# Four-layer 56x56 image kernel: layer 1's last image stored by quarters, other buffers for layer 0's images, first group's channels of two convolutions stored and loaded ahead of the rest

## The chip, the cores and the metric

The kernel runs on one core of one Trainium2 chip. The metric is the device time of one execution in microseconds. The core has five engines, each with its own instruction stream: TensorE (PE in the profile; PEld are its weight loads), VectorE (DVE), ScalarE (ACT), GpSimd (POOL) and SyncE (SP). Data move between DRAM and the on-chip memory (SBUF) by DMAs, which SP, ACT and POOL issue. A DMA that an engine issues stands in that engine's stream, so it goes out only after everything ahead of it there. All queues share the core's 16 DMA engines.

## The reference

The input is 8 images of 56 x 56 pixels with 192 channels, float32. Four layers follow each other, each with a residual:

```
x = x + L0(gn(x))   # p * (toeplitz over w and over h of q*v), then a projection
x = x + L1(gn(x))   # window attention, 7x7 windows shifted by 3, 6 heads
x = x + L2(gn(x))   # projection to 384, 3x3 depthwise conv, decays in 4 directions, projection
x = x + L3(gn(x))   # 7x7 depthwise conv, layer norm, GELU MLP, scaled
```

`gn` is a group norm over each image (32 groups of 6 channels), so no layer can start on an image before that image is finished in the layer before. The shift by 3 rolls the image by three rows and three columns, both when layer 1 reads and when it writes.

## The kernel before

The work is done in stages, one after the other over all 8 images: layer 0's first phase (q and v), layer 0's mixing, layer 1, layer 2's projection in, layer 2's mixing (384 channels in groups of 16), layer 2's projection out with layer 3's input, layer 3's depthwise convolution (192 channels in groups of 16), and layer 3's MLP. Between stages the data go through DRAM: `x1` and `x2` are the images that enter layers 1 and 2, `pd` the projected images of layer 2, `zd` the inputs of layer 3's convolution. Inside a stage a framework adds the waits that data and buffers need and schedules each engine's order of instructions; SP's, ACT's and POOL's DMAs have their places in these streams. Every stage takes its tiles from pools that reuse the memory of earlier stages; a tile that lies on an older tile waits until the readers of that one, its DMAs too, have finished. The program keeps at most eight DMAs of SP and ACT together outstanding: each waits for the one eight before it.

An image lies in a tile of 128 partitions as two halves (partitions 0 to 63 the upper 28 rows, 64 to 127 the lower), with three blocks `j` of 64 channels.

- **Layer 0's mixing** (`layer0_mix`, from L462). Images are loaded into `x0` tiles (L468), the first before anything else; the products of the Toeplitz rows are copied to `o` (L529, first `o` tile allocated at L522), each image is normalized to `xn` (L474), and an image is stored to `x1` by two DMAs (L481). Behind the last products `loaded()` (L1193) opens a pool of three layer-1 image tiles at the end of the memory and loads images 0 and 1 into it.
- **Layer 1.** `layer1_load` calls `rolled` (L590), which loads an image in 18 DMAs (L598): rows and columns are rolled, so a DMA moves runs of 53 or of 3 elements. An image has 128 x 3 x 28 x 2 = 21,504 such runs, about 2.4 MB. `layer1_norm` writes normalized windows to `xr` (L619), takes their mean with a matmul (L626) and squares (L630); `layer1_weights` folds vectors into the weights (L567, L578), for which POOL has loaded `w_qkv` and `w_proj`. Image b is then done in four quarters `g` of 7 rows each half: scores and softmax, with a mask tile `bm` loaded on SP (L693), then the mix, which adds its result to the image tile in place (L767). After the four quarters the image is stored to `x2` by 18 DMAs (`rolled`, L598). The next images' norms run ahead of time in between.
- **Layer 2's projection in** (`layer2_in`, from L770) for each image: POOL clears borders of an `x2` tile (L774, L775), SP loads the image in two DMAs (L777, L778), DVE normalizes it into `xn` in three instructions (L783), POOL clears borders of `xn` (L786, L787), TensorE projects (`pin`, L795), DVE adds the bias `b_in` into `pt` (L803), and SP stores `pt` to `pd[b]` (5.57 MB, L804). The two `x2` tiles lie on layer 1's image tiles. POOL loads `w_in` and `b_in` (L97) ahead of the first image.
- **Layer 2's mixing** (`layer2_mix`). For a group of 16 channels SP loads the band weights `wt` (2.05 MB, L825) and the group's channels of all 8 images (`zc`, eight DMAs of 0.23 MB, L830); TensorE convolves four channels at a time (`cv`, L839). Two groups' tiles are in flight.
- **Layer 3's convolution** (`convolve`) has the same form with `wt` of 4.2 MB (L1004), `zc` of eight times 0.25 MB (L1009) and TensorE's `cps` (L1016).

## Time and profile before

| | us |
|---|---|
| median of 3 runs | 6279.67 (6277.85 to 6285.88) |
| the profiled execution | 6264.17 |
| its span in the trace | 6262.4 |
| TensorE busy | 5524.5 (88%) |
| VectorE busy | 3441.0 (55%) |
| ScalarE busy | 2243.7 (36%) |
| GpSimd busy | 1312.8 (21%) |

Approximate stages in the trace, with TensorE's busy time:

| stage | window, us | TensorE busy, us |
|---|---|---|
| layer 0, first phase | 60 to 867 | 739.4 |
| layer 0, mixing | 867 to 2137 | 1166.8 |
| layer 1 | 2137 to 3610 | 1194.3 |
| layer 2, projection in | 3610 to 3854 | 242.2 |
| layer 2, mixing | 3854 to 4480 | 590.8 |
| layer 2, projection out | 4480 to 5064 | 431.8 |
| layer 3, convolution | 5064 to 5376 | 299.9 |
| layer 3, MLP | 5376 to 6262 | 830.6 |

In the lines of the trace the first number is the start in us from the span's start, the second the busy time, then the engine, the line of the source, the operation, the tile written and the tiles read, how many instructions the row joins, and in brackets the idle time of the engine before the row and what ended it. A row that begins with SPq is SP's queue issuing DMAs; its time runs from the first issue to the last, waits between them included. Times of the profiled execution can't be laid beside the median directly: this execution was 15.5 us below it.

### The profile page before, as it was taken

How to read it: one execution, taken by the hardware profiler on the slowest of the kernel's cores; microseconds unless marked ns; L12 is line 12 of the kernel's file. 1: busy time of each engine (PE TensorE's matmuls, PEld its weight loads, DVE VectorE, ACT ScalarE, POOL GpSimd, SP SyncE). 2: the span in 40 equal slices, each digit the busy share in tenths (PEclk: the TensorE clock that was granted, in tenths of full speed). 3: DMA queues.
4: the chain of work that ended last, by engine and by line, in shares of the span. 5: the costliest groups of instructions: out<-in, count | busy, mean ns of one | idle time of the engine just before them, and what ended most of it. 6: DMA issues, size and time to landing. Idle time of an engine off the chain costs nothing. (4 is left out here: it accounts for less than half of the span.)

```text
span 6262.4 us, 126450 instructions
## 1 busy us (share of the span) xinstructions
PE 5524.5 (88%) x55636; PEld 3577.2 (57%) x55636; DVE 3441.0 (55%) x4776; ACT 2243.7 (36%) x2929; POOL 1312.8 (21%) x833
## 2 busy tenths in 40 slices
PE   6899989999999788888888698999688879799999
PEld 5677766666666355445454365777444479544444
DVE  5677766556555344444444386888787710433331
ACT  2334444344444233333333200555355510233333
POOL 1100025444444021121221101333200100110100
PEclk8899999999999798888888798999889989899999
DMA  6799986666665514444432395666666578422210
GB/s 165 188 220 207 192 246 262 256 253 259 254 260 208 77 33 64 56 64 60 59 50 39 55 259 224 215 220 232 190 164 198 165 292 330 154 80 67 71 58 24
DMA packets 1039757, 1013.11 MB, mean 162 GB/s; under 512 B 832281, under 2 KB 964549, under 8 KB 1012325
## 3 DMA queue, kind: packets, MB, share of 16 engines
q1 hardware_dynamic: 1027920, 951.41, 53.6%
q0 software_dynamic: 6416, 34.07, 1.6%
q10 hardware_dynamic: 4868, 19.52, 0.9%
q8 instruction: 437, 7.16, 0.5%
q14 instruction: 116, 0.94, 0.0%
HBM read 676.28 MB, written 345.08 MB: 163 GB/s over the span
## 5 line engine op out<-in xcount | busy, mean ns | idle before, releaser
L371 PE MATMUL qv<-w_qv_sb,xn 64*112 64x288 f32 x5376 | 724.0, 426 | 48.4 <-DVE act L377 45.2
L409 POOL COPY lc<-lt 128x896 f32<-128x896 f32 (+1 forms) x320 | 575.8, 1816 | 623.6 <-PE op L417 605.8
L371 PEld LDWEIGHTS qv<-w_qv_sb,xn 64*112 64x112 f32 x5376 | 534.8, 184 | 232.3 <-DVE act L377 61.2
L378 ACT ACTIVATE act<-act 112x576 f32<-112x576 f32 x448 | 299.5, 682 | 463.0 <-DVE act L377 421.3
L1115 PE MATMUL ph<-y,w_sb 64*128 64x392 f32 x2304 | 399.2, 499 | 6.4 <-ACT hid L1119 6.4
L417 PE MATMUL op<-rc,lc 128*56 128x56 f32 x9216 | 344.1, 223 | 54.4 <-POOL lc L409 29.7
L417 PEld LDWEIGHTS op<-rc,lc 128*56 128x56 f32 x9216 | 312.7, 138 | 137.4 <-issue 72.2
L1126 PE MATMUL po<-hid,w_sb 128*64 128x392 f32 x2304 | 386.3, 494 | 0.0
L429 PE MATMUL pj<-xn,w_p_sb 64*128 64x392 f32 (+1 forms) x1920 | 374.2, 516 | 8.4 <-issue 5.6
L450 PE MATMUL y<-pp,w_o_sb 128*64 128x392 f32 (+1 forms) x1920 | 356.1, 504 | 14.8 <-DVE x L456 6.6
L377 DVE TENSOR_TENSOR act<-qv,b_qv 112x576 f32<-112x576 f32 x448 | 320.5, 750 | 85.5 <-PE qv L371 85.3
L1133 DVE TENSOR_TENSOR x<-x,z 128x392 f32<-128x392 f32 x96 | 72.3, 753 | 520.8 <-ACT z L1131 520.8
L409 ACT COPY rc<-rt 128x896 f32<-128x896 f32 (+1 forms) x160 | 256.8, 1606 | 239.4 <-PE op L417 218.6
L839 PE MATMUL cv<-zc,wt 128*128 128x224 f32 x1536 | 312.8, 355 | 27.9 <-DMA zc<-pd 27.9
L710 POOL TENSOR_TENSOR e<-e,mx 128x1176 f32<-128x1176 f32 x64 | 139.8, 2185 | 920.4 <-DVE mx L709 920.4
L839 PEld LDWEIGHTS cv<-zc,wt 128*128 128x128 f32 x1536 | 290.5, 189 | 71.0 <-issue 54.9
L443 DVE TENSOR_TENSOR pp<-pp,ot 128x784 f32<-128x784 f32 (+1 forms) x160 | 154.6, 966 | 312.8 <-ACT pp L434 293.0
L660 PE MATMUL qk_ps<-xr,wg 64*96 64x392 f32 x1536 | 310.8, 513 | 14.8 <-ACT qk L666 13.3
L1016 PE MATMUL cps<-zc,wt 128*128 128x224 f32 x1536 | 299.9, 356 | 25.3 <-DMA zc<-zd 24.4
L1115 PEld LDWEIGHTS ph<-y,w_sb 64*128 64x128 f32 x2304 | 220.8, 189 | 176.7 <-issue 26.8
L1016 PEld LDWEIGHTS cps<-zc,wt 128*128 128x128 f32 x1536 | 290.0, 189 | 35.2 <-issue 27.5
L852 POOL TENSOR_TENSOR rows<-rows,loc 128x896 f32<-128x896 f32 x96 | 228.3, 2378 | 389.7 <-ACT rows L848 262.4
(207 smaller groups left out, 9293.2 us busy)
## 6 DMA issues: line engine op xcount, KB each, us to landing
lt<-left SPq DMA_DIRECT2D x72, 1792.0 KB
rt<-right SPq DMA_DIRECT2D x72, 1792.0 KB
left<-qv SPq DMA_DIRECT2D x224, 252.0 KB
right<-qv SPq DMA_DIRECT2D x448, 126.0 KB
wt<-in_band_dram SPq DMA_DIRECT2D x24, 2048.0 KB
wt<-in_band_dram SPq DMA_DIRECT2D x12, 4096.0 KB
pd<-pt SPq DMA_DIRECT2D x8, 5568.0 KB
zc<-pd SPq DMA_DIRECT2D x192, 232.0 KB
```

The lines of the kernel that those rows point to most:

```text
L371: nc.tensor.matmul(ps[s][:, which, 0:D1 // 2], xn[64 * s:64 * s + 64, j, bass.ts(i, 2 * W)], w_qv[64 * s:64 * s + 64, j, which, ns], start ...
L377: nc.vector.tensor_tensor(act, ps[s][:, :, 0:D1 // 2], b_qv[:, :, ns], ALU.add)
L378: nc.scalar.activation(act, act, AF.Silu)
L409: copy(c[:, 0:nu], raw.rearrange("p (w u d) -> p u d w", u=nu, d=64 // nu)[:, :, d0:d0 + 8])
L417: nc.tensor.matmul(op[64 * u:64 * u + W, i, :], lc[:, u, i], rc[:, u, i], start=True, stop=True)
L429: nc.tensor.matmul(ps[0:M, s, 0:TT], w_p[64 * s:64 * s + 64, j, d0:d0 + M], xn[64 * s:64 * s + 64, j, ts], start=(j == 0), stop=(j == 2),)
L450: nc.tensor.matmul(y[64 * s:64 * s + 64], w_o[0:M, c, 64 * j:64 * j + 64], pp[0:M, s], start=(c == gated[0][0]), stop=(c == gated[-1][0]),)
L660: nc.tensor.matmul(ps[s], wg[64 * s:64 * s + 64, j, c0:c0 + HC], xw[64 * s:64 * s + 64, j, gs], start=(j == 0), stop=(j == 2),)
L839: nc.tensor.matmul(dst, wt[:, c4 + i, 128 * q:128 * q + 128], zc[:, :, c4 + i, q:q + NPAIR], start=(q == 0), stop=(q == 1),)
L1016: nc.tensor.matmul(dst.rearrange("p (b n) -> p b n", n=NPAIR), wt[:, c4 + i, q * OP:(q + 1) * OP], zc[:, :, c4 + i, q:q + NPAIR], start=(q ...
L1115: nc.tensor.matmul(ps[:, s, 0:TT], w0[64 * s:64 * s + 64, j, m * 128:(m + 1) * 128], y[64 * s:64 * s + 64, j, ts], start=(j == 0), stop=(j ...
L1126: nc.tensor.matmul(ps[64 * s:64 * s + 64], w1[:, m, 64 * j:64 * j + 64], hid[:, m, s], start=(m == 0), stop=(m == 5),)
```

## The change

1. Layer 0's mixing allocates and loads its first image only after the first operand copies and the first `o` tile. The pools place tiles in the order of allocation, so the `x0` tiles move up in memory (their base goes from 32,736 to 108,000 bytes in a partition) and `o` and the operands move down.
2. The layer-1 pool opens with a dummy tile (8 images over 3 buffers). Image 0's loads go out on two queues, block `j` 0 and 2 on SP and 1 on POOL. Image 1's loads are written later in the source, after image 0's norm; in the streams, ten of its 18 loads now stand ahead of the last store of layer 0 and eight behind it.
3. Layer 1's last image is stored in quarters by the new `rolled_rows`, after each quarter's mix: 12, 12, 12 and 18 DMAs on SP.
4. `layer2_in` is split: `layer2_image` allocates, clears and loads. Image 0's load goes to POOL's queue, ahead of `w_in` and `b_in`, which go to ACT's queue. Image b + 1 is asked for before image b is projected. In DVE's stream the first of the three L783 instructions of image 1 now stands ahead of those of image 0, and the other two directly behind them.
5. `pd` of the last image is stored in two DMAs, its first 16 channels (0.24 MB) and the rest. In both convolutions, the first group loads `wt` for 4 channels, then `zc` over three queues (images 0, 3, 6 on SP, 1, 4, 7 on POOL, 2, 5 on ACT), then `wt` for the other 12.

TensorE's stream has the same instructions in the same order as before.

```diff
@@ -482,7 +482,7 @@
                     x1[b].rearrange("(j p) n -> p j n", p=64)[:, :, s * NH:(s + 1) * NH], x[64 * s:64 * s + 64]
                 )
 
-        x, xn, gate, left_over, st = [load(0)], None, iter(()), 0, None
+        x, xn, gate, left_over, st = [], None, iter(()), 0, None
 
         todo = [
             (b, s, d0, len(chunks)) for b in range(nimg) for chunks, subs in PASSES for s in subs
@@ -520,6 +520,9 @@
                         done[1] += 1
 
                 o = pool.tile([120, H, 128], F32, name="o")
+                if not x:
+
+                    x.append(load(0))
                 for at in range(0, 64 // nu * len(subs), 8):
                     right_operand()
                     layer0_products(ops[n % 2], nu, lcs[n], rcs[n])
@@ -587,19 +590,33 @@
         nc.vector.tensor_scalar(wg[:, :, 0:C], wg[:, :, 0:C], HD ** -0.5, None, ALU.mult)
         return wg, bq, w_proj, bpr
 
-    def rolled(dram_image, tile_image, store):
+    def rolled(dram_image, tile_image, store, queues=(nc.sync,)):
 
         d = dram_image.rearrange("(j p) (h w) -> p j h w", p=64, w=W)
         for s, h0, h1, r0 in ((0, 0, 28, 3), (1, 0, 25, 31), (1, 25, 28, 0)):
             for w0, w1, c0 in ((0, 53, 3), (53, 56, 0)):
                 for j in range(3):
+                    eng = queues[j % len(queues)]
                     sb = tile_image[64 * s:64 * s + 64, j, h0:h1, w0:w1]
                     dr = d[:, j, r0:r0 + h1 - h0, c0:c0 + w1 - w0]
-                    nc.sync.dma_start(dr, sb) if store else nc.sync.dma_start(sb, dr)
-
-    def layer1_load(b, pool):
+                    eng.dma_start(dr, sb) if store else eng.dma_start(sb, dr)
+
+    def rolled_rows(dram_image, tile_image, g):
+
+        d = dram_image.rearrange("(j p) (h w) -> p j h w", p=64, w=W)
+        for s in range(2):
+            for h0, h1 in ((7 * g, 7 * g + 7),) if (s, g) != (1, 3) else ((21, 25), (25, 28)):
+                r0 = (28 * s + h0 + 3) % H
+                for w0, w1, c0 in ((0, 53, 3), (53, 56, 0)):
+                    for j in range(3):
+                        nc.sync.dma_start(
+                            d[:, j, r0:r0 + h1 - h0, c0:c0 + w1 - w0],
+                            tile_image[64 * s:64 * s + 64, j, h0:h1, w0:w1],
+                        )
+
+    def layer1_load(b, pool, queues=(nc.sync,)):
         x = pool.tile([128, 3, H // 2, W], F32, name="x1")
-        rolled(x1[b], x, False)
+        rolled(x1[b], x, False, queues)
         return x
 
     def layer1_norm(b, x, pool, psum, consts):
@@ -767,15 +784,18 @@
             nc.vector.scalar_tensor_tensor(xs, ps, bpr[:, j:j + 1], xs, ALU.add, ALU.add)
 
 
-    def layer2_in(b, pool, xpool, psum, w_in, b_in):
-
+    def layer2_image(b, xpool, queue):
 
         x = xpool.tile([128, 3, R2, W], F32, name="x2")
         nc.gpsimd.memset(x[0:64, :, 0], 0.0)
         nc.gpsimd.memset(x[64:128, :, R2 - 3:R2], 0.0)
         src = x2[b].rearrange("(j p) (h w) -> p j h w", p=64, w=W)
-        nc.sync.dma_start(x[0:64, :, 1:R2], src[:, :, 0:R2 - 1])
-        nc.sync.dma_start(x[64:128, :, 0:R2 - 3], src[:, :, R2 - 1:H])
+        queue.dma_start(x[0:64, :, 1:R2], src[:, :, 0:R2 - 1])
+        queue.dma_start(x[64:128, :, 0:R2 - 3], src[:, :, R2 - 1:H])
+        return x
+
+    def layer2_in(b, x, pool, psum, w_in, b_in):
+
         sc, sh = scsh2[:, b, 0], scsh2[:, b, 1]
         xn = pool.tile([128, 3, R2, 64], F32, name="xn2")
         nc.gpsimd.memset(xn[:, :, :, W:64], 0.0)
@@ -801,7 +821,11 @@
             dims = [list(z) for z in pt.ap]
             dst = bass.AP(pt.tensor, pt.offset + i, [dims[0], [nh, ns], [P2, C2]])
             nc.vector.tensor_tensor(dst, ps[:, 0:ns, 0:C2], b_in[:, v, 0:ns], ALU.add)
-        nc.sync.dma_start(pd[b], pt)
+
+        n = CG2 if b + 1 == nimg else 0
+        if n:
+            nc.sync.dma_start(pd[b][:, 0:n], pt[:, 0:n])
+        nc.sync.dma_start(pd[b][:, n:C2], pt[:, n:C2])
 
     def layer2_mix():
 
@@ -822,12 +846,15 @@
             def load(g):
                 cs = slice(g * CG2, (g + 1) * CG2)
                 wt = pool.tile([128, CG2, 256], F32, name="wt2")
-                nc.sync.dma_start(
-                    wt, bass.AP(band.tensor, band.offset + g * CG2 * BL2, [[1, 128], [BL2, CG2], [1, 256]])
-                )
+                src = bass.AP(band.tensor, band.offset + g * CG2 * BL2, [[1, 128], [BL2, CG2], [1, 256]])
+
+                n, queues = (CG2, (nc.sync,)) if g else (4, (nc.sync, nc.gpsimd, nc.scalar))
+                nc.sync.dma_start(wt[:, 0:n], src[:, 0:n])
                 zc = pool.tile([128, nimg, CG2, P2], F32, name="zc2")
                 for b in range(nimg):
-                    nc.sync.dma_start(zc[:, b], pd[b][:, cs])
+                    queues[b % len(queues)].dma_start(zc[:, b], pd[b][:, cs])
+                if n < CG2:
+                    nc.sync.dma_start(wt[:, n:CG2], src[:, n:CG2])
                 return wt, zc
 
             def front(c4, wt, zc, loc, rows, sums):
@@ -1001,12 +1028,15 @@
             for g in range(C // CG):
                 cs = slice(g * CG, g * CG + CG)
                 wt = pool.tile([OP, CG, BAND], F32, name="wt")
-                nc.sync.dma_start(
-                    wt, bass.AP(band.tensor, band.offset + g * CG * BL, [[1, OP], [BL, CG], [1, BAND]])
-                )
+                src = bass.AP(band.tensor, band.offset + g * CG * BL, [[1, OP], [BL, CG], [1, BAND]])
+
+                n, queues = (CG, (nc.sync,)) if g else (4, (nc.sync, nc.gpsimd, nc.scalar))
+                nc.sync.dma_start(wt[:, 0:n], src[:, 0:n])
                 zc = pool.tile([OP, nimg, CG, NB], F32, name="zc")
                 for b in range(nimg):
-                    nc.sync.dma_start(zc[:, b], zd[b][:, cs])
+                    queues[b % len(queues)].dma_start(zc[:, b], zd[b][:, cs])
+                if n < CG:
+                    nc.sync.dma_start(wt[:, n:CG], src[:, n:CG])
                 yc = pool.tile([OP, nimg, CG, NPAIR], F32, name="yc")
                 for c4 in range(0, CG, 4):
                     ps = psum.tile([OP, 2, 512], F32, name="cps")
@@ -1194,7 +1224,10 @@
             raws.close()
             xpool = images.enter_context(tc.tile_pool(reuse_waits="tile", name="l1x", bufs=3, side="right"))
             x.append(xpool)
-            x.extend(layer1_load(b, xpool) for b in range(min(2, nimg)))
+
+            for _ in range(-nimg % 3):
+                xpool.tile([128, 3, H // 2, W], F32, name="x1")
+            x.append(layer1_load(0, xpool, (nc.sync, nc.gpsimd)))
 
         layer0_mix(pool, blocks, psum, ops, w_p, w_o, loaded)
 
@@ -1225,6 +1258,8 @@
         xr = [next(steps)]
         for _ in steps:
             pass
+        if nimg > 1:
+            x.append(layer1_load(1, xpool))
         values = layer1_scores(0, xr[0], pool, psum, S, es, consts)
 
 
@@ -1258,9 +1293,12 @@
                 layer1_mix(g, x[b], values, pool, psum, es, consts)
                 values = following
                 gn_piece(gn[b], x[b].rearrange("p j h w -> p j (h w)"), g)
+                if b + 1 == nimg:
+                    rolled_rows(x2[b], x[b], g)
             for _ in steps:
                 pass
-            rolled(x2[b], x[b], True)
+            if b + 1 < nimg:
+                rolled(x2[b], x[b], True)
         gn_aggregate(gn[nimg - 1], mv2[:, nimg - 1])
     images.close()
 
@@ -1269,10 +1307,13 @@
         xpool = st.enter_context(tc.tile_pool(reuse_waits="tile", name="l2x", bufs=2, side="right"))
         pool = st.enter_context(tc.tile_pool(reuse_waits="tile", name="l2i", bufs=2))
         psum = st.enter_context(tc.tile_pool(reuse_waits="tile", name="l2ip", bufs=4, space=PSUM))
-        w_in = resident("w_in", nc.gpsimd, pool)
-        b_in = resident("b_in", nc.gpsimd, pool)
+        x = [layer2_image(0, xpool, nc.gpsimd)]
+        w_in = resident("w_in", nc.scalar, pool)
+        b_in = resident("b_in", nc.scalar, pool)
         for b in range(nimg):
-            layer2_in(b, pool, xpool, psum, w_in, b_in)
+            if b + 1 < nimg:
+                x.append(layer2_image(b + 1, xpool, nc.sync))
+            layer2_in(b, x[b], pool, psum, w_in, b_in)
             if b == nimg - 3:
                 run(gn_finish(mv2[:, last], scsh2[:, last, 0], scsh2[:, last, 1], pool, psum, "pin"))
     layer2_mix()
```

## The prediction

> **What bounds the kernel now.** I read the page's shares first, then the windows by stage, then the timeline around each place that the diff touches, because the change removes no arithmetic: it can only shorten stretches in which the engines wait.
>
> ```profile
> PE 5524.5 (88%) x55636; PEld 3577.2 (57%) x55636; DVE 3441.0 (55%) x4776; ACT 2243.7 (36%) x2929; POOL 1312.8 (21%) x833
> ...
> PEclk8899999999999798888888798999889989899999
> ```
>
> TensorE is busy for 88% of the 6262.4 us span, so some 740 us are idle, and its clock drops to 0.7 in slices 14 and 23. Those slices hold the seams between stages. The timeline (start, duration, engine, line, what, idle before and its releaser) shows five of them. Seam A, from layer 0's first phase to its mixing:
>
> ```profile
> 881.31 0.63 DVE L529 COPY o<-op 120x448 f32<-120x448 f32 x1 [5.53 <-DMA right<-qv]
> ...
> 882.08 3.24 PE L417 MATMUL op<-rc,lc 128*56 128x56 f32 x64 [3.76 <-DVE o L529]
> ...
> 889.74 1.10 DVE L474 TENSOR_SCALAR xn<-x,scsh 128x1568 f32<-128x1568 f32 x1 [6.95 <-DMA x<-in_x_dram]
> ```
>
> Seam B, layer 0 to layer 1:
>
> ```profile
> 2068.63 53.64 SPq L598 DMA_DIRECT2D x<-x  x36
> ...
> 2107.90 4.00 PE L567 MATMUL bias<-vecs_sb,w_qkv_sb 64*96 64x1 f32 x24 [1.39 <-DMA w_qkv_sb<-in_w_qkv_dram]
> ...
> 2122.37 1.24 SPq L481 DMA_DIRECT2D x<-x  x2
> ...
> 2135.87 4.55 ACT L619 ACTIVATE xr<-x,scsh 128x392 f32<-128x392 f32 x7 [32.82 <-DMA x<-x]
> ...
> 2136.71 3.60 PE L626 MATMUL mean<-xr,ones 128*128 128x392 f32 x5 [22.24 <-issue]
> ```
>
> Image 7's store (L481) is ready at 2107.1, when its last addition ends, but stands behind 36 image loads on SP's queue. The first xr and the e memset wait for it, since their memory is image 7's old tile. Seam C, layer 1 to layer 2:
>
> ```profile
> 3555.59 35.66 SPq L598 DMA_DIRECT2D x<-x  x18
> ...
> 3591.64 0.59 SPq L777 DMA_DIRECT2D x<-x  x1
> ...
> 3606.77 3.28 DVE L783 TENSOR_SCALAR xn<-x,scsh 128x1680 f32<-128x1680 f32 x3 [47.57 <-DMA x<-x]
> ...
> 3610.40 2.29 PE L795 MATMUL pin<-w_in_sb,xn 64*128 64x384 f32 x6 [52.87 <-POOL xn L786]
> ```
>
> Image 7's 18 stores end TensorE's work for 52.87 us: image 0's two loads queue behind them. Seams D and E, projection to mixing and layer 2 to layer 3's convolution:
>
> ```profile
> 3854.38 0.32 SPq L804 DMA_DIRECT2D pd<-pt  x1
> 3854.86 0.39 SPq L825 DMA_DIRECT2D wt<-in_band_dram  x1
> 3855.43 20.98 SPq L830 DMA_DIRECT2D zc<-pd  x8
> ...
> 3881.36 2.95 PE L839 MATMUL cv<-zc,wt 128*128 128x224 f32 x7 [27.89 <-DMA zc<-pd]
> ```
>
> ```profile
> 5044.42 0.38 SPq L1004 DMA_DIRECT2D wt<-in_band_dram  x1
> 5044.86 14.92 SPq L1009 DMA_DIRECT2D zc<-zd  x8
> ...
> 5064.91 3.33 PE L1016 MATMUL cps<-zc,wt 128*128 128x224 f32 x8 [22.43 <-DMA zc<-zd]
> ```
>
> Both first groups wait for everything in front of them to move. The windows give 388 GB/s from 3855 to 3877 and 364 from 5045 to 5060, with all DMA engines busy.
>
> **What the Trainium skill says.** "DMA: Bandwidth & Descriptors", section "Issuing engines are not separate DMA queues": DMAs started by different engines run on the same 16 DMA engines and interleave, and spreading them saves only the issuing time. Its section "Queues, rings and completion order" adds that each DMA engine takes turns between queues, packet by packet. So at D and E I price bytes, not queues, but let the other two queues get past a long transfer on SP's. The trace before has no such mixture. Its section "Anatomy of one DMA — SWDGE (gpsimd) path" says of GpSimd's descriptors that their cost is "small, variable" and shows only after many; the trace bounds it below. "TensorE: Matmul & The Clock Gate", Part 1, says that the array runs at half clock for some microseconds after idling; the trace agrees (a convolution matmul takes up to 711 ns, median 354).
>
> **A, 0 to +3 us, taken +2.** The new order puts x0 over the memory of the qv tiles and the o tiles elsewhere. The o copies lose their wait (3.76 us of TensorE), but the first x0 load now waits for the qv stores that held them, until about 881.3; it was issued at 879.09. The normalization at 889.74 needs this load and gates the first pj matmul at 890.94. So the gain is swallowed and 2.2 us are lost. If the stores end sooner, nothing.
>
> **B, taken −18.** Before image 7's store SP now holds 12 loads of image 0 and 10 of image 1, not 36; six of image 0 go to POOL's queue. The 36 loads took 53.64 us for 43,008 runs of 53 or 3 elements, 802 a us. The store can issue once 14 of SP's 22 are through (8 are outstanding at most in the program), with POOL's 7,168 runs: 25,088 runs, 31 us, so about 2100: it goes at 2107.2, when its data is there. Its 2.41 MB at 388 GB/s need 6 us, and image 1's last eight loads follow. xr and e no longer lie on that tile, so the first mean could start when the bias matmuls end (2114.5). But on ACT three xr of image 1 stand ahead of image 0's first square, and their loads are two behind the store: about 2118, instead of 2136. Cheapest case −22. What is late next is image 1's last pieces (about 2120), then nothing: bm loads stand behind them as before.
>
> The unknown is POOL's descriptors: 7,168 in six DMAs, in front of w_qkv. The groups of POOL's DMAs show the nearest rows:
>
> ```profile
> L328 POOL DMA_DIRECT2D mk<-in_mask_dram x16: 742/762/789, 48.5 to 290.8; - x16
> ...
> DMA to landing us min/median/max: 2.5/5.3/9.8
> ```
>
> A mask load of 196 runs holds POOL 0.76 us, a rel load of 49 runs 0.58 and lands in 1.9 (least 1.8). From the issue times a run costs 1.3 ns; from the least landings (2.5 − 1.8)/147 = 4.8; from the medians (5.3 − 1.9)/147 = 23, which holds other traffic's share. That makes 9, 34 or 165 us. I take up to 34: from 2068.6 it ends at 2103, w_qkv (2102.4 before) is hardly moved.
>
> **C, −10 to −33, taken −27.** Image 7's stores become 54 in quarters. The first three hide under the mixing of the later quarters; only the last 18, 5,376 runs, stand after the last addition at 3558.3. The 18 whole stores needed 40.2 us (3555.59 to the release of their tile at 3595.74) for 21,504 runs, 535 a us: 10 us here, so 3566 to 3569. Image 0's loads are on POOL, free to go near 3547, w_in and b_in on ACT. But in the program that is built, DVE's first L783 instruction belongs to image 1, whose tile is image 7's: its load on SP waits until all of image 7 is stored. So image 0's early load doesn't set the start. Image 1's 2.4 MB take about 6 + 2 us, 3578.5; image 1's first normalization (1.1), image 0's three (3.3) and the memset put the first projection at 3583, instead of 3610.4. Two more of image 1 (2.2 us) stand before the first pt, which had 4.25 us; covered by four PSUM buffers. b_in, sent after the last addition, lands in about 9.8 us, before it is needed. Ends: the load takes 15.1 us as image 0's did, −20; stores paced by count as in the second rival, −10; all faster, −33.
>
> **D, −8 to 0, taken −4.5.** Last zc (L830) could go only when image 7's whole 5.57 MB store was down (3876.4), and landed 5 us later behind wt. Now it needs the first 16 channels' 0.24 MB. In front of the first four channels stand 5.7 MB of store, 0.5 of wt and 1.86 of zc, 7.9 MB: 20.4 us from 3854.5 plus 2 to land, 3877. (The same sum for before, 9.5 MB, gives 3881.) The other 12 channels' wt (1.5 MB) comes 3.9 us later, and four channels take TensorE 3.3 (16 matmuls), more when cold. POOL's dec memset (3.09 us) stands before its zc and is covered.
>
> **E, −10 to −3, taken −7.** First four channels need 1.05 MB of wt and 2.03 of zc: 8.5 us + 2 to 3.4 (before, 6.2 MB, needed 17 + 3.4), about 5056 instead of 5064.9. They take 6.2 us (24.9 for a group, the rate afterwards), cold up to twice; the rest of wt lands at 5064. The group ends at 5083, not 5090; the second group's data (12.4 MB) is in at 5081.
>
> **Sum.** +2 − 18 − 27 − 4.5 − 7 = −54.5. The profiled execution took 6264.2, so 6209.7; the median of the runs shown lies 15.5 above it, so 6225.
>
> **Rivals.**
> - POOL writes descriptors slowly enough that image 0 lands as late as before (9.4 ns a run, 67 us): B gives nothing, 6243. For it: the medians above. Against: the issue times.
> - The quarter stores are paced by their number: 18 in 35.66 us is 1.98 us each; 15 after 3558.4 then end at 3593, C gives 2 or so, 6250. For it: eight outstanding. Against: a DMA is a quarter as large, and the rate by runs (535 and 802 a us) fits large and small ones.
> - Slower than before: the first mechanism, stronger. A, C, D and E save 36.5 together, so image 0 must land 36.5 after 2135.8: from 103.7 us for 7,168 runs, 14.5 ns each, it decides. At 23 ns it lands at 2234, +98: 6341.
> - Queues interleave better: POOL's and ACT's zc pass the long store at D (−8), E −10, C −33, B −22, A 0: 6207.
> - Waits only move and nothing is measured: layer 1 refills it. Little speaks for it; DVE is busy 0.44 there. 6275.
>
> **How the numbers follow.** The main case has 0.60, slow descriptors 0.10, paced stores 0.10, slower 0.05, better interleaving 0.12, nothing 0.03. The measurement can tell about 0.2%, 12.6 us: faster 0.92, same 0.03, slower 0.05. All but the last two cases lie between 6207 and 6250; bounds added, 6200 to 6252.
>
> **What would show it.** B: first mean near 2118, image 7's store issued at 2107 rather than 2122, POOL's DMA times near 0.8 us. C: 18 last stores in 10 us, DVE's first L803 waiting for a SP load, first projection at 3583. D: first cv near 3877; E: first cps near 5056 and a stall before its fifth channel under 3 us. A: the wait before pj longer by 2. The prediction is wrong if POOL's loads land after 2135, or stores of a quarter take as long as whole ones.

## The result, and the profile after

The changed kernel took 6243.88 us (median of 6 runs, 6225.77 to 6253.75), the kernel before in the same set 6280.91 (6 runs, 6277.85 to 6301.1): a ratio of 0.9932 (95% interval 0.9912 to 0.9952). The forecast was 6225 (6200 to 6252). The direction and the range held; the time was 19 us above the forecast. The profiled execution took 6248.97 us, its span 6247.2, which is 15.2 us less than the span before, where the runs differ by 37. So two things are to be found: where 19 us of the forecast gain went, and why this one profile shows so little.

The page of the changed kernel, busy times, slices and granted clock, says again that no arithmetic was removed:

```profile
PE 5524.0 (88%) x55636; PEld 3580.0 (57%) x55636; DVE 3453.0 (55%) x4776; ACT 2244.2 (36%) x2929; POOL 1318.7 (21%) x845
...
PEclk8899999999999888888888798999889989899999
```

TensorE is busy for 5524.0 us, 0.5 less than before. The gain is in its waits. In the timelines below the columns are as in the prediction. Seam A, from layer 0's first phase to its mixing, changed kernel:

```profile
874.32 0.62 DVE L532 COPY o<-op 120x448 f32<-120x448 f32 x1 [1.08 <-PE op L417]
...
887.52 1.10 DVE L474 TENSOR_SCALAR xn<-x,scsh 128x1568 f32<-128x1568 f32 x1 [10.56 <-DMA x<-in_x_dram]
```

The `o` copy no longer waits for a DMA, and the first normalization waits 10.56 us for x0 instead of 6.95, as forecast. Seam B, layer 0 to layer 1, changed kernel:

```profile
2057.41 43.40 SPq L602 DMA_DIRECT2D x<-x  x22
2059.42 5.37 POOL L602 DMA_DIRECT2D x<-x  x6 [2.04 <-issue]
...
2096.55 4.00 PE L570 MATMUL bias<-vecs_sb,w_qkv_sb 64*96 64x1 f32 x24 [1.26 <-DMA w_qkv_sb<-in_w_qkv_dram]
2100.91 2.88 SPq L481 DMA_DIRECT2D x<-x  x2
2103.83 15.45 SPq L602 DMA_DIRECT2D x<-x  x8
...
2106.65 0.74 ACT L636 ACTIVATE xr<-x,scsh 128x392 f32<-128x392 f32 x1 [10.97 <-DMA x<-x]
2117.24 1.38 ACT L636 ACTIVATE xr<-x,scsh 128x392 f32<-128x392 f32 x2 [9.85 <-DMA x<-x]
2118.52 1.17 ACT L647 ACTIVATE sq<-xr 128x1176 f32<-128x1176 f32 x1
```

The bias matmuls start earlier and the first mean follows 10.3 us after layer 0's last matmul (30.2 before), but ACT waits twice for the last loads of image 1 (10.97 and 9.85 us) ahead of the first square. Eight of these stand behind image 7's store on SP (L602 at 2103.83). Seam C, layer 1 to layer 2, changed kernel; layer 1's last addition ends at 3563.6:

```profile
3548.48 39.72 SPq L612 DMA_DIRECT2D x<-x  x30
3558.12 0.67 POOL L793 DMA_DIRECT2D x<-x  x1
...
3589.65 0.59 SPq L793 DMA_DIRECT2D x<-x  x1
...
3604.17 6.49 DVE L803 TENSOR_SCALAR xn<-x,scsh 128x1680 f32<-128x1680 f32 x6 [39.65 <-DMA x<-x]
...
3609.82 2.93 PE L815 MATMUL pin<-w_in_sb,xn 64*128 64x384 f32 x8 [46.98 <-POOL xn L806]
```

The wait that stood here before (52.87 us) is 46.98: this is where the forecast gain is missing. The last quarters' stores run on until 24 us after the last addition, not 10. Seams D and E, changed kernel:

```profile
3876.43 14.58 PE L866 MATMUL cv<-zc,wt 128*128 128x224 f32 x64 [24.49 <-DMA zc<-pd]
...
5051.60 38.70 PE L1046 MATMUL cps<-zc,wt 128*128 128x224 f32 x190 [15.28 <-DMA zc<-zd]
```

The waits are 24.49 us (27.89 before) and 15.28 (22.43 before). Neither row is broken at the fifth channel: 64 and 190 matmuls run on.

The table gives these stretches in four profiled executions. `Again 1` and `again 2` are two more executions of the changed kernel, from the experiments below.

| us | before | after | again 1 | again 2 |
|---|---|---|---|---|
| A: first op matmul to first pj matmul | 15.9 | 16.2 | 16.0 | 17.7 |
| B: layer 0's last matmul to first mean | 30.2 | 10.3 | 10.3 | 10.3 |
| B: the same to first square | 36.0 | 23.2 | 24.3 | 22.7 |
| B: the same to layer 1's first addition | 138.4 | 120.1 | 123.6 | 125.9 |
| layer 1: first addition of image 0 to that of image 7 | 1215.6 | 1252.2 | 1219.2 | 1235.3 |
| C: last addition to first projection | 52.1 | 46.2 | 44.6 | 45.1 |
| D: last projection to first cv | 27.9 | 24.5 | 24.2 | 24.2 |
| E: last cv to last cps | 901.0 | 892.0 | 892.6 | 892.5 |

The five seams (A, B at the first addition, C, D, E) sum to −36, −34 and −30 us in the three executions of the changed kernel. The medians of the three sets differ by 37, 27 and 36. The first profile hides the gain in one row: layer 1 between the two additions, whose instructions are the same, took 36.6 us more there. That it still gained 15.2 comes from stretches outside the table, most of it from layer 0's mixing behind its first pj matmul (1206.6 us after 1215.6; 1200 to 1216 over all profiles kept). In layer 1 the other two executions took 3.6 and 19.7 more.

### The profile page after: what moved, and what is told of

The parts are those of the page before. It is cut to its first block, busy times and chain, and to the rows that moved or that the text cites. A ratio compares the mean times of both kernels' runs of the same rounds, so it can differ in the third digit from the quotient of the medians.

```text
span 6247.2 us, 126516 instructions
## 1 busy us (share of the span) xinstructions
PE 5524.0 (88%) x55636; PEld 3580.0 (57%) x55636; DVE 3453.0 (55%) x4776; ACT 2244.2 (36%) x2929; POOL 1318.7 (21%) x845
## 5 line engine op out<-in xcount | busy, mean ns | idle before, releaser
L727 POOL TENSOR_TENSOR e<-e,mx 128x1176 f32<-128x1176 f32 x64 | 139.8, 2185 | 956.8 <-DVE mx L726 935.6
L866 PE MATMUL cv<-zc,wt 128*128 128x224 f32 x1536 | 312.6, 355 | 24.5 <-DMA zc<-pd 24.5
```

The lines of the kernel that those rows point to most:

```text
L866: nc.tensor.matmul(dst, wt[:, c4 + i, 128 * q:128 * q + 128], zc[:, :, c4 + i, q:q + NPAIR], start=(q == 0), stop=(q == 1),)
```

## The experiments

Each set of four ran on one chip beside the kernel before, and the three sets on three chips. The kernel before took 6257.93, 6266.82 and 6272.06 us there, so ratios are compared across sets, not times.

**Again, and layer 1's pace.** Two rival accounts of the 36.6 us: the pace of layer 1's transfers belongs to the execution (P), or the change slows layer 1, for instance by its new tile places (R).

> The changed kernel once more, unaltered. Its first profiled execution gained 29.5 us by layer 1's first quarter and lost 35 of it inside layer 1, where the 36 transfers that follow an image's end took 67 to 70 us instead of 62 to 64. Theory P (the pace of these transfers belongs to the execution or to where the program's data lie, not to the edit): time between 6225 and 6254 us again, the 36 transfers anywhere from 62 to 70 us, and an execution with short ones is shorter by some 3 us an image. Rival R (the edit slows layer 1): the transfers take 67 to 70 us again, an image 177 to 180 us, and the lead is lost by image 6.

Measured: 6230.91 us, ratio 0.9960 (0.9948 to 0.9973). An image's 36 transfers (18 stores, 18 loads) took 63.5 to 64.5 us, in the first profile of the same kernel 67.5 to 70.2, before 62.1 to 63.7. R asks for the long ones in every execution of the changed kernel; in this form it falls.

> The changed kernel once more, unaltered, beside the three that follow. First projection 44 to 47 us after the last addition of layer 1, first square 23 to 25 after layer 0's last addition. Theory P (the pace of layer 1's short runs belongs to the execution and not to the edit): all four kernels of this set show a common length of an image's 36 transfers, within 2 us of each other where the 36 are on the same queue; the rival (the change itself slows layer 1): 67 us or more here, whatever the others show.

Measured: 6236.35 us, 0.9944 (0.9930 to 0.9957). The transfers took 64.6 to 66.9 us, and 65.4 to 67.6 in the next two kernels of that set, which have them on the same queue. The kernels of this set agree within 2 us, as P asks. Over the thirteen profiles with these transfers, of both kernels and the variants below, layer 1 takes 1216 to 1230 us at 61 to 65 us for the transfers, 1225 to 1246 at 65 to 68, and 1252 at 69: they go together, but 20 us of spread remain at one pace. What makes TensorE wait in that time was not settled. Nor is a small slowing by the edit excluded. The three profiles with the old start of layer 1 took 1216 to 1224 us, the ten with the new one 1219 to 1252; but eight of the ten are from other chips or the first profile, and on the one chip that has both kinds they overlap (1218 and 1224 against 1219 and 1230).

**The parts alone.** Each part was put into the kernel before. First parts 1 and 2 of the change, layer 0's images and layer 1's first loads:

```diff
-        x, xn, gate, left_over, st = [load(0)], None, iter(()), 0, None
+        x, xn, gate, left_over, st = [], None, iter(()), 0, None
...
+                if not x:
+                    x.append(load(0))
...
-            x.extend(layer1_load(b, xpool) for b in range(min(2, nimg)))
+            for _ in range(-nimg % 3):
+                xpool.tile([128, 3, H // 2, W], F32, name="x1")
+            x.append(layer1_load(0, xpool, (nc.sync, nc.gpsimd)))
...
+        if nimg > 1:
+            x.append(layer1_load(1, xpool))
```

> The kernel before with the change's first two parts alone: x0 tiles moved, image 0's layer-1 loads on two queues, image 1's loads later. Both theories: first mean of layer 1 near 2105 to 2118 instead of 2136.7. Theory P: the lead of 18 to 30 us at layer 1's first quarter is kept as far as the transfers keep 63 us, so 6250 to 6263. Rival R (this part makes layer 1 slower): the lead is gone by image 7, 6278 to 6284.

Measured: 0.9983 (0.9976 to 0.9991). First mean 10.3 after layer 0's last matmul, first square 24.6: the gain of B is 11 to 15 us and needs nothing of the other parts.

Then parts 3 and 4 alone, the end of layer 1:

```diff
+                if b + 1 == nimg:
+                    rolled_rows(x2[b], x[b], g)
...
-        w_in = resident("w_in", nc.gpsimd, pool)
-        b_in = resident("b_in", nc.gpsimd, pool)
+        x = [layer2_image(0, xpool, nc.gpsimd)]
+        w_in = resident("w_in", nc.scalar, pool)
+        b_in = resident("b_in", nc.scalar, pool)
```

> The kernel before with the change's parts 3 and 4 alone: last image stored in quarters, layer 2's images loaded ahead, image 0's on POOL, w_in and b_in on ACT. The prediction's step: 18 last stores in 10 us and the first projection 27 us earlier, 6254. What the changed kernel's trace suggests instead (theory S): image 0's 2.4 MB on POOL's queue go out at the same moment as the last quarters' stores and hold them up, the last 18 stores end some 25 us after the last addition, image 1's load takes 14 us, and the first projection starts about 46 us after the last addition instead of 52: 6275.

Measured: 0.9984 (0.9975 to 0.9993). First projection 45.4 us after the last addition, 52.1 before: C gives 7 us whatever stands around it.

Then part 5 alone, here its lines for layer 2's mixing; layer 3's convolution has the same:

```diff
+        n = CG2 if b + 1 == nimg else 0
+        if n:
+            nc.sync.dma_start(pd[b][:, 0:n], pt[:, 0:n])
...
+                n, queues = (CG2, (nc.sync,)) if g else (4, (nc.sync, nc.gpsimd, nc.scalar))
+                nc.sync.dma_start(wt[:, 0:n], src[:, 0:n])
...
+                    queues[b % len(queues)].dma_start(zc[:, b], pd[b][:, cs])
+                if n < CG2:
+                    nc.sync.dma_start(wt[:, n:CG2], src[:, n:CG2])
```

> The kernel before with the change's part 5 alone: first channels of both convolutions stored and loaded ahead. The prediction's steps D and E: 4.5 and 7, so 6269. What the changed kernel's trace suggests: first convolution matmul of layer 2 3.5 to 5 us earlier after the last projection and that of layer 3 about 8 earlier, 6267 to 6270. If the other queues' share is what makes it, nothing in layers 0 and 1 differs from before.

Measured: 0.9976 (0.9966 to 0.9986). First cv 24.0 us after the last projection, last cv to last cps 892.8: D −3.9 and E −8.2. The three ratios make −10.6, −10.0 and −15.0 us of 6257.93, −36 together, against −25 for the whole by its ratio in that set; intervals of 5 to 6 us to either side of each leave room for that. A's stretch was 14.3 and 14.1 us in the last two kernels, whose code there is that of the kernel before, and 16.0 in the first.

**C: what slows the last stores.** In `again 1` the last addition ends at 3545.2. The DMA queues of that execution, first while only stores run (3535 to 3541), then for eleven us beside image 0's load (3542 to 3553), then after it (3554 to 3559); columns are packets, MB and share of the 16 engines' time:

```profile
q1 hardware_dynamic: 3534, 0.37, 45.2%
...
q0 software_dynamic: 322, 1.93, 76.2%
q10 hardware_dynamic: 144, 0.59, 23.0%
q1 hardware_dynamic: 308, 0.00, 2.6%
...
q1 hardware_dynamic: 3178, 0.36, 74.4%
```

SP's stores (q1) move 3534 packets, nearly all of them single runs, in six us, then 308 in eleven, then 3178 in five: 589, 28 and 636 a us. In between, POOL's queue (q0) moves pieces of 6496 and 6048 bytes, some 440 ns each, and ACT's (q10) w_in in pieces of 4608. In the Trainium skill, "DMA: Bandwidth & Descriptors", section "Queues, rings and completion order", each DMA engine takes turns between queues packet by packet. The trace agrees: 308 packets of SP's queue, each one run of 12 bytes, went against 322 of POOL's. A second stop is `b_in`, on ACT's queue: in the first profile of the changed kernel its pieces of 9216 bytes went out 14.9 to 21.1 us after the last addition, and SP's queue moved 16 packets from 3578 to 3583. Three edits of the changed kernel each alter one part of this. First, image 0's load stands behind the stores, on SP:

```diff
-        x = [layer2_image(0, xpool, nc.gpsimd)]
+        x = [layer2_image(0, xpool, nc.sync)]
```

> The changed kernel with one word changed: layer 2's image 0 is loaded on SP's queue, behind the last quarters' stores, instead of POOL's. Theory S (in the changed kernel that 2.4 MB load goes out at the same moment as the stores' short runs, and these hardly move until it has landed): the stores are issued to their end about 10 us after the last addition instead of 24. The scheduler also puts image 0's normalization first here, so the first projection starts some 27 us after the last addition instead of 45: 15 to 18 us faster than the changed kernel. Rival N (the stores are slow by their number, 54): still issued to their end 20 us or more after the last addition, first projection 38 us or more after it, no gain on the changed kernel.

Measured: 6224.64 us, 0.9935 (0.9922 to 0.9948). Without the load beside them the last stores were issued 12.4 us after the last addition, instead of 22 to 24, and the first projection came at 31.1, though image 0's load was issued 13 us after the last addition and no longer 5 ahead of it:

```profile
3575.04 0.59 SPq L793 DMA_DIRECT2D x<-x  x1
...
3589.43 3.29 DVE L803 TENSOR_SCALAR xn<-x,scsh 128x1680 f32<-128x1680 f32 x3 [26.55 <-DMA x<-x]
...
3593.06 19.27 PE L815 MATMUL pin<-w_in_sb,xn 64*128 64x384 f32 x100 [31.86 <-POOL xn L806]
```

Three normalizations of image 0 alone stand ahead here, six of both images in the changed kernel; so this kernel changes the order on DVE as well. The crawl beside image 0's load is worth 10 to 12 us of the stores' end; what it alone is worth at the first projection this kernel doesn't show. The whole is not clear of the changed kernel, whose ratios were 0.9932 to 0.9960; layer 1 took 1246 us in this profile.

Second, the last quarter's stores go on POOL, ahead of image 0's load:

```diff
-                        nc.sync.dma_start(
+                        (nc.gpsimd if g == 3 else nc.sync).dma_start(
```

> The changed kernel with the last quarter's 18 stores on POOL's queue, where the trace shows packets of up to 20 runs joined. They stand ahead of image 0's load there. Theory S: short runs on SP's queue alone crawl beside long pieces; joined ones don't, and the image is stored some 18 us after the last addition (18 instructions of 0.7 to 0.9 us), image 1's load is issued then instead of at 24, and 4 to 7 us are gained. Rival N (number of DMAs): 18 more instructions on POOL take as long as on SP, no gain.

Measured: 6229.36 us, 0.9945 (0.9929 to 0.9961). The last store was issued at 12.1 us and had landed at 13.9, but the first projection came at 44.2, so the expected 4 to 7 us were not gained. Both images' loads, 4.8 MB, then went out together near 14, and POOL's two landed 16.3 and 24.1 us after their issue. DVE, which takes image 1 first, waited for both images.

Third, the load stays and the quarters go: all 18 whole stores after the last addition.

```diff
-                if b + 1 == nimg:
-                    rolled_rows(x2[b], x[b], g)
...
-            if b + 1 < nimg:
-                rolled(x2[b], x[b], True)
+            rolled(x2[b], x[b], True)
```

> The changed kernel with the last image of layer 1 stored whole, by 18 DMAs after its last addition, as before. If image 0's early load on POOL starves short runs wherever they stand beside it, the 18 whole stores end later than the 32 us of the kernel before, at 35 to 45 after the last addition, and the first projection comes 58 to 68 after it, against 52 before and 45 with quarters: 13 to 23 us slower than the changed kernel and no gain at this seam without the quarters. If the quarters are worth only the runs that they take off the end, 16,128 runs at 590 a us are 27 us. If they are worth nothing, because image 1's load sets the start anyway, the first projection stays at 44 to 47.

Measured: 6249.54 us, 0.9959 (0.9943 to 0.9975), 13 us more than the changed kernel of that set. The last store was issued 45.4 us after the last addition, where the kernel before needed 32.3, and the first projection followed at 69.9, a little beyond what the first theory gave:

```profile
3535.03 48.77 SPq L602 DMA_DIRECT2D x<-x  x18
...
3607.61 4.64 PE L802 MATMUL pin<-w_in_sb,xn 64*128 64x384 f32 x16 [70.64 <-POOL xn L793]
```

So C holds two effects of opposite sign: the quarters take 24.8 us off (69.9 to 45.1), and the rest of C puts 17.8 us on (52.1 to 69.9). The forecast put the second at nothing. The median moved by 13 and not 25; in the two profiles layer 1 took 10 us less here (1225 and 1235), by a spread that stays open.

**C: the order on DVE and POOL.** In the changed kernel the first of image 1's three normalizations stands ahead of image 0's on DVE, and POOL's clear of image 1's tile, which waits for that tile's stores, ahead of the clear of `xn` for image 0. First DVE's order alone was written out, with image 0's normalization, then ten `pt`, then image 1's (`between`):

```diff
+        st.enter_context(tc.manual_schedule(engines={mybir.EngineType.DVE}))
+        x.append(layer2_image(1, xpool, nc.sync))
+        xn = [layer2_normed(0, x[0], pool)]
...
-            layer2_in(b, x[b], pool, psum, w_in, b_in)
+            layer2_in(b, xn[b], pool, psum, w_in, b_in, between)
```

> The changed kernel with DVE's order in layer 2's projection written out: image 0's three normalizations first, image 1's after ten bias additions. Image 0 stays on POOL's queue. Theory O (the order on DVE decides: the first projection waits for image 1, whose tile waits for the last stores): the stores end as late as in the changed kernel (24 us after the last addition), but the first projection starts 15 to 18 us after the last addition instead of 45, and 25 to 28 us are gained on the changed kernel, unless image 1 stops it later. If the order doesn't matter: no gain.

Measured: 6216.70 us, 0.9921 (0.9909 to 0.9933). Image 0's normalization started at 11.8 us, but the first projection came at 25.9, not by 18:

```profile
3562.44 3.28 DVE L803 TENSOR_SCALAR xn<-x,scsh 128x1680 f32<-128x1680 f32 x3 [10.88 <-DMA x<-x]
...
3575.48 0.23 POOL L790 MEMSET x<- 64x168 f32 x1 [29.05 <-DMA x<-x]
...
3576.32 0.23 POOL L806 MEMSET xn<- 64x168 f32 x1
...
3576.60 35.71 PE L821 MATMUL pin<-w_in_sb,xn 64*128 64x384 f32 x202 [26.73 <-POOL xn L806]
```

POOL waits 29.05 us at L790 until image 7 is stored, and the clear of `xn` (L806) that the projection needs stands behind it.

Then both orders were written out, and image 1 of layer 1 loaded on POOL as well:

```diff
-            x.append(layer1_load(1, xpool))
+            x.append(layer1_load(1, xpool, (nc.gpsimd,)))
...
+        st.enter_context(tc.manual_schedule(engines={mybir.EngineType.DVE, mybir.EngineType.Pool}))
+        xn = [layer2_normed(0, x[0], pool)]
+        x.append(layer2_image(1, xpool, nc.sync))
```

> The changed kernel with the order of DVE and of POOL at the start of layer 2's projection written out (image 0 first on both, image 1's clears and normalization behind it) and image 1 of layer 1 loaded on POOL. If the remaining 11 us between image 0's normalization and the first projection were POOL's clear of image 1's tile standing ahead of the clear of xn, the first projection comes 15 to 18 us after the last addition (45 and 26 in the kernels before it), then a stall of up to 10 us for image 1 later, which it needs only 30 us on. First square 15 to 17 after layer 0's last addition, against 23 to 25. Together 30 to 38 us below the changed kernel of this set. If another thing holds the projection (the b_in load, the last stores), it stays at 24 to 27, and the whole is 22 to 28 below.

Measured: 6210.06 us, 0.9894 (0.9877 to 0.9911), 26 us below the changed kernel of that set. First projection 15.0 us after the last addition (3551.4), as forecast:

```profile
3566.17 0.23 POOL L806 MEMSET xn<- 64x168 f32 x1 [19.56 <-DVE xn L803]
...
3566.45 29.81 PE L821 MATMUL pin<-w_in_sb,xn 64*128 64x384 f32 x168 [15.78 <-POOL xn L806]
3596.69 9.94 PE L821 MATMUL pin<-w_in_sb,xn 64*128 64x384 f32 x54 [0.44 <-DVE pt L829]
```

The clear now follows the normalization, and image 1 holds the stream nowhere: its first break is 0.44 us, for `pt`. At this seam the kernel gains 30.1 us on the changed kernel of its set, at layer 1's first addition 10.0 (first square at 17.5); 10 us are gone again in layer 1 (1242 us instead of 1235, and 3 more in image 7). The two profiled executions lie 34 us apart, the medians 26, short of the expected 30 to 38. The stores crawled here too, the last one issued at 23.7 us: once nothing ahead of the first projection waits for them, their crawl costs the start nothing. It is the fastest kernel here; its interval just meets that of the one before.

**B: the loads beside image 7's store.**

```diff
-            x.append(layer1_load(1, xpool))
+            x.append(layer1_load(1, xpool, (nc.gpsimd,)))
```

> The changed kernel with layer 1's image 1 loaded on POOL's queue instead of SP's, so that none of its pieces stands behind image 7's store. In the changed kernel the first mean starts 10 us after layer 0's last matmul, but the first square 23 to 25 after it, since three instructions ahead of it on ACT wait for pieces of image 1 that crawl beside the store. Theory S: first square 12 to 14 us after layer 0's last matmul and the first addition of layer 1 some 10 us earlier, 5 to 11 us faster than the changed kernel. If POOL is slow at writing the 21,504 runs (14 ns a run or more): the first mean itself is late and the time is above the changed kernel's.

Measured: 6233.47 us, 0.9940 (0.9924 to 0.9956). The first square came 16.1 us after layer 0's last matmul, 7 to 8 us sooner than in the changed kernel (12 to 14 were expected), and layer 1's first addition at 117.3 (120 to 126 in the changed kernel). So image 1's last loads were what held ACT; the whole kernel is not measurably faster than the others of its set.

**Layer 1's loads on POOL.**

```diff
-                    x.append(layer1_load(b + 2, xpool))
+                    x.append(layer1_load(b + 2, xpool, (nc.gpsimd,)))
```

> The changed kernel with images 2 to 7 of layer 1 loaded by POOL instead of SP; the stores stay on SP. POOL's queue joins short runs, so the 18 loads should take under 20 us beside 18 stores of 34 us, and an image's transfers end 25 to 30 us sooner. If the stalls of TensorE in layer 1 come from the time in which short runs keep the DMA engines busy (theory: 5 us an image between paces of 63 and 69 us), layer 1 from its first quarter to image 7's first quarter is 20 to 30 us shorter than in the unaltered kernel of this set. If they come from the order of the instructions or from something that only goes with the pace, it is the same within 8 us. Against both: POOL waits at the first load for the image before to be stored, and what stands behind it on POOL waits as well; then layer 1 is longer.

Measured: 6285.15 us, 1.0024 (1.0013 to 1.0034), slower than the kernel before. DVE's and POOL's timelines:

```profile
2597.14 1.38 DVE L726 TENSOR_REDUCE mx<-e 128x24 f32<-128x1176 f32 x1
...
2609.28 1.07 POOL L602 DMA_DIRECT2D x<-x  x1 [43.48 <-DMA x<-x]
2610.36 2.20 POOL L727 TENSOR_TENSOR e<-e,mx 128x1176 f32<-128x1176 f32 x1
...
2627.83 11.54 POOL L602 DMA_DIRECT2D x<-x  x13
```

POOL waits 43.48 us for the stores of the image whose tile is loaded, and a step of the softmax (L727), ready when DVE's maximum (L726) ended at 2598.5, starts at 2610.36 behind it. Thirteen more loads then hold POOL for 11.54 us. The edit also let image 2's 18 loads go ahead in the seam to layer 1, where image 1's then landed later (first square at 43.0). The loads took 32 us (2612 to 2644), not under 20, with other work of POOL between their issues. So this kernel shows what a waiting DMA does to what is behind it; it doesn't tell what makes layer 1 wait at a slow pace, which stays open.

## Why the prediction was right in sign and short in size

- **A, taken +2.** Against the one profile before, the three executions took 0.1 to 1.9 us more. Over all profiles kept, the eleven kernels with part 1 took 15.6 to 18.1 us (mean 16.6), the three without it 14.1 to 15.9 (mean 14.7): +1.9, as forecast. The mechanism shows: the `o` copies lost their wait and the wait for x0 grew.
- **B, taken −18.** The first mean came as forecast, 10.3 us after layer 0's last matmul (11.5 by the forecast's 2118). The first square gained 12 to 13 only. What failed is the time of "the store can issue once 14 of SP's 22 are through": 31 us were counted from the first load, and it took 43.5. So the store was issued 5 us after its data was there, and then image 1's last eight loads, of which the prediction had ACT wait for two, took 12.5 to 15.5 us to issue, beside a store whose 6272-byte pieces were under way until 2115.1, 11 us where 6 were counted; in the trace before they took 11 too (2123.6 to 2135.0). The prediction saw this as the next thing late ("about 2120") and priced it at nothing. Layer 1's first addition still gained 12 to 18.
- **POOL's price** (9, 34 or 165 us, "I take up to 34") came out near its low end: the six DMAs were issued in 5.37 us, 0.9 each, and landed 8.8 to 10.2 us after issue. The first and the third rival, both of slow descriptors, fell by this; that the measured 6243.88 is the first rival's number, 6243, is coincidence, since that rival has B give nothing and C its full 27. In the Trainium skill, "DMA: Bandwidth & Descriptors", section "Anatomy of one DMA — SWDGE (gpsimd) path", the cost of descriptors is called small, and the trace agrees.
- **C, taken −27, measured −6 to −7.5.** This is the failed step, and it is about all of the 19 us. Two terms of its sum were mis-sized. "18 last stores … 10 us here" took the rate of stores that run alone; they took 22 to 24, since image 0's load, priced as costing them nothing, and `b_in` went out beside them (with whole stores the last one went out 13 us later, 45.4 and 32.3). And "image 1's 2.4 MB take about 6 + 2 us" were 14.5 us from issue to normalization (3589.65 to 3604.17); the 15.1 that the trace before showed for image 0 was put in the range only. That DVE's first normalization belongs to image 1 was in the prediction, and was left as a given; by the runs above, it and POOL's clear cost 30 us.

  "The trace before has no such mixture" was wrong, and the sign of the crawl could be read there. From 2104 to 2106.5, while POOL's `w_qkv` came in (q0), SP's image loads (q1) came to a near stop; from 2101 to 2103.5 the same queue had moved 2919 packets:

```profile
q0 software_dynamic: 119, 0.81, 87.7%
q1 hardware_dynamic: 3, 0.00, 0.1%
```

  The second rival's value (−2) was nearer, but its mechanism is not what happens: a quarter's twelve stores took 8.4 to 9.8 us where no load ran beside them, 0.7 to 0.8 each, not 1.98.
- **D, taken −4.5, and E, taken −7**: −3.4 to −3.9 and −8 to −9. Bytes ahead at the rate of the windows gave both to 2 us; no fifth-channel stall was seen.
- **"Waits only move"**: three executions of the changed kernel took 36.6, 3.6 and 19.7 us more in layer 1 than the one profile of the kernel before. The medians kept the gain of the seams, so this rival fell in the main. The kernel before itself has one profile; with the two kernels above that keep its start of layer 1 the spread is 8 us.

With the measured terms the forecast's sum would have been +2 −15 −7 −4 −8 = −32, about 6248 beside the medians shown before, against 6243.88.

## What to carry to other kernels

Before a load is moved ahead of stores on another queue, look at the size of the pieces on both: here a queue of short runs got one run, or less, for each long piece of the other, so the early load is paid for by what must finish first. Then follow the order on each engine to the instruction that starts the next stage: it starts with the latest thing queued ahead of it, here another image's normalization on one engine and a clear on another, and not with its own data. And profile a changed kernel more than once before explaining a stage whose code is the same.

## What the runs showed of the hardware

- Short runs beside long pieces: 589 and 636 packets a us alone, 28 beside pieces of about 440 ns (C above), and 3 in 2.5 us beside `w_qkv` in the trace before.
- POOL's queue joins short runs into packets, SP's doesn't. In the changed kernel's seam B, POOL's six loads of 7,168 runs are in here:

```profile
q1 hardware_dynamic: 32064, 5.15, 75.2%
q0 software_dynamic: 592, 1.90, 16.5%
```

  592 packets in all, with those of `w_qkv`, `w_proj` and `sel`; 160 of them of 4,240 bytes, which is 20 runs of 212. They took 523 ns on average, 26 a run, and single runs of 212 bytes on SP's queue 25 in the same stretch, so joining did not move a run faster. Whether it helps beside long pieces is not shown: with the last quarter on POOL, its queue moved 2 packets from 3542 to 3546, beside `b_in`.
- The same 36 transfers on the same queue took 61 to 70 us of an image's time, steady within an execution (1 to 3 us between images): 61 to 65 on one chip, 65 to 68 on two others, 62 to 64 and 67 to 70 in the two profiles before the experiments. What sets it stays open.
